# Layer 0 of a four-layer AdaLN/FFN kernel: a copy moved to VectorE, constants computed per group, two stores moved, and unread transposes added on TensorE

## The chip, the cores and the metric

The kernel runs on one core of one Trainium2 chip. A core has five engines that run their own instruction streams and wait for one another only through semaphores: TensorE (PE in the profile, with its weight loads as a row of their own, PEld), VectorE (DVE), ScalarE (ACT), GpSimd (POOL) and SyncE (SP). SP, ACT and POOL also issue DMA transfers. The metric is the device time of one execution in microseconds; lower is better. A difference under about 0.3% (5.7 us here) can't be told from no change.

## The reference

Four layers follow one another, each `x = x + ffn(cond(x))`, with x of 32 sequences x 64 positions x 256 features, so 2048 rows. All data are float32. The change touches layer 0 alone:

```python
def _L0_cond_ref(hidden_states, activation, W_q, b_q, W_kv, b_kv, no_op_k, no_op_v, W_proj, b_proj):
    q = hidden_states @ W_q + b_q                      # heads: 16 of 16 features
    kv = activation @ W_kv + b_kv                      # one key and one value per sequence
    k = concatenate([no_op_k, k1]); v = concatenate([no_op_v, v1])
    w = softmax(einsum('bhsd,bhkd->bhsk', q, k))       # two keys only
    return einsum('bhsk,bhkd->bhsd', w, v) @ W_proj + b_proj

def _L0_ffn_ref(x, router_w, router_b, w1, b1, w2, b2):
    gates = softmax(x @ router_w + router_b)           # 8 experts, the best 2 of each row
    # each expert takes at most capacity = 320 rows, in the order of the rows
    out = gelu(rows @ w1[e] + b1[e]) @ w2[e] + b2[e]
    y = sum over experts of gate * out
```

There are only two keys per head, so the softmax depends on one difference: score = q . (k1 - no_op_k). With W_q folded into that difference, it is x . A plus a constant per sequence and head, where the constant is b_q . (k1 - no_op_k).

## The kernel before

A library schedules the program: it follows the program order and dependencies with its own estimate of the times and writes a fixed order for each engine; within that order every engine waits for what it needs. `tc.issue_after(mark)` adds one rule: what is traced in its block on the engine of `mark` is placed behind `mark` in that engine's order. It is an order of issue, no wait.

Layer 0 runs in these stages. `constants` (L148) makes the identity and turns the condition rows; SiLU of them is the first thing that ACT computes. `fold_loads` (L675) and the loop at L829 issue the first loads: Wq, Wkv and the four pieces of X (512 KB each) from ACT, the small ones from SP. The hardware transfers use eight completion counters in turn, and an issue waits until the last user of its counter has landed.

`fold_scores` (L704) makes `kx`, the key differences spread over heads (L736), turns Wq with four transposes (`transposed`, L119, called at L743), copies the turned leaves out of the PSUM bank (`wqT`), multiplies them with `kx` into A (L752), and computes the constants of all four groups of rows at once with sixteen narrow matmul records (L758) into `z0`. The same loop then makes `vx` for the values. `evacuate` (L106) gives its copies to ACT and to DVE by turns; the count runs through the first three layers.

Then comes a loop over four groups of four tiles of 128 rows (L833): X is turned (`tile_features`, L127, copies on ACT), the scores are made by L841, `z0` is added on DVE (L846, L847), and the weights `at_w` follow by two exponentials on ACT and four DVE instructions. `fold_output` (L780) folds W_proj and the router into `M` (wpT copied by `evacuate`, L791, L796, L801, L809).

The next loop over groups (L858 on) makes the rows of the table: matmuls L866 and L867, a copy to C on ACT (L868), the softmax of the gates on DVE, and a store of 528 KB per group from SP (L872). Behind the loop in program order SP stores X into `acc` (L878, 2048 KB, and L879, 128 KB), and ACT fills `acc_c` with zeros (L884, 2176 KB). Nothing ties these three to the table loop, so the scheduler issued them as soon as X had landed.

`routed` (L451) runs the experts. `slots` (L361) finds which rows each expert takes: `positions` (L307) by two matmuls, then one-hot planes on DVE (L357) and sixteen narrow fp16 matmuls per expert (L397); ACT writes the row numbers (L401). POOL gathers the expert's rows from the table with indirect DMAs (L473, three per expert), which need all four table stores to have landed; PE turns them (L481), and the expert's matmuls run (L438, L447). While this goes on SP loads pieces of the last layer's weights (L1399, 176 KB each over 88 partitions, and L1403) and later experts' weights.

PSUM holds four one-bank buffers (`bank`) and two of two banks (`wide`); a new tile takes the buffer that was released first.

## Time and profile before

| what | value |
|---|---|
| median of three runs | 1898.23 us (1897.44 to 1902.32) |
| the profiled execution | 1896.54 us, of which the span is 1894.8 us |
| PE busy | 1546.4 us, 82% of the span |
| PEld busy | 1191.3 us, 63% |
| DVE, ACT, POOL busy | 712.0, 600.8, 569.4 us |
| mean granted TensorE clock | 0.873 |
| first matmul of the first expert (L438) | at 74.13 us |
| POOL's first gather from the table (L473) | at 65.75 us |

A row of the timeline reads: start in us, length in us, engine, line, operation, output<-input, shapes, number of merged instructions, and in brackets the idle time before it and what ended that. A q behind an engine's name is its sequencer issuing transfers. A row of a stretch's sums reads: bounds, length, then per engine the busy time and the number of instructions, the granted clock, the DMA engines' busy share and GB/s.

### The profile page before, as it was taken

The numbers are of one execution on the slowest core, as the hardware profiler recorded it, in microseconds if no ns is written. First come the engines' busy times: TensorE is split into PE (matmuls) and PEld (weight loads), VectorE is DVE, ScalarE is ACT, GpSimd is POOL, SyncE is SP. The second block draws the span as 40 slices with busy tenths as digits, with TensorE's granted clock in tenths as the row PEclk, the third lists the DMA queues.
The fourth block names the chain that finished last, engine by engine and source line by source line (L and its number), as shares of the span: only waits on it lengthen the run. The fifth ranks groups of instructions, "written<-read, shape, count | busy, mean of one in ns | idle before, by whom it ended". The sixth has DMA issues, their size and how long they took to land.

```text
span 1894.8 us, 26736 instructions
## 1 busy us (share of the span) xinstructions
PE 1546.4 (82%) x9935; PEld 1191.3 (63%) x9935; DVE 712.0 (38%) x2402; ACT 600.8 (32%) x1308; POOL 569.4 (30%) x740
## 2 busy tenths in 40 slices
PE   6799998999987839999675499999665669878767
PEld 5576767888876738888564366667543446546445
DVE  3782043111101161111213601000456668777765
ACT  2222332333331203333211022222134455545443
POOL 0233310233320013332100223331235445455452
PEclk9799998999997959999885599999867778788789
DMA  7455542566632046666511044442310100100000
GB/s 262 139 153 136 137 117 60 171 194 178 179 95 86 6 157 172 179 181 164 152 26 25 24 107 129 105 112 64 115 32 22 46 17 23 32 14 32 14 12 11
DMA packets 158406, 183.81 MB, mean 97 GB/s; under 512 B 37540, under 2 KB 137536, under 8 KB 158272
## 3 DMA queue, kind: packets, MB, share of 16 engines
q1 hardware_dynamic: 123920, 143.34, 23.7%
q0 software_dynamic: 21248, 29.24, 8.9%
q10 hardware_dynamic: 13104, 9.47, 1.6%
q8 instruction: 81, 1.33, 0.3%
q14 instruction: 53, 0.43, 0.1%
HBM read 152.22 MB, written 29.79 MB: 96 GB/s over the span
## 4 chain that ended last, share of the span: by engine, by line
PE 26%; DVE 9%; POOL 6%; issue 5%; ACT 4%; DMA 1%; SPq 0%; POOLq 0%; DVEq 0%
PE bank L438 6%; PE bank L447 6%; PE bank L1133 3%; PE bank L1877 2%; PE bank L1761 2%; PE bank L1684 1%; PE bank L1894 1%; PE bank L1458 1%; PE bank L1795 1%; ACT squares L1603 1%; PE bank L1596 1%; PE wide L1145 1%; DVE mag L1360 1%; POOL mb_root L147 1%; POOL mag L1353 1%
## 5 line engine op out<-in xcount | busy, mean ns | idle before, releaser
L447 PE MATMUL bank<-w,hidden 128*128 128x256 f32 (+1 forms) x2080 | 458.7, 379 | 0.0
L447 PEld LDWEIGHTS bank<-w,hidden 128*128 128x128 f32 (+1 forms) x2080 | 387.8, 187 | 66.2 <-issue 6.5
L438 PE MATMUL bank<-xeT,w 128*128 128x256 f32 (+2 forms) x1440 | 400.1, 437 | 25.2 <-ACT xeT L110 22.2
L438 PEld LDWEIGHTS bank<-xeT,w 128*128 128x128 f32 x1440 | 275.5, 194 | 137.9 <-issue 65.2
L626 DVE TENSOR_TENSOR y<-bank,b 128x256 f32<-128x256 f32 x58 | 24.6, 425 | 361.0 <-PE bank L447 361.0
L440 ACT ACTIVATE hidden<-bank,ge_cols 128x256 f32<-128x256 f32 x232 | 109.8, 473 | 114.7 <-PE bank L438 114.7
L489 DVE TENSOR_TENSOR y<-bank,b 128x256 f32<-128x256 f32 (+1 forms) x56 | 23.6, 422 | 304.5 <-PE bank L447 304.5
L440 ACT ACTIVATE hidden<-bank,bias_cols_b 128x256 f32<-128x256 f32 (+1 forms) x128 | 73.7, 580 | 122.7 <-PE bank L438 118.3
L491 POOL DMA_INDIRECT acc<-y,l2f_add x32 | 50.6, 1582 | 161.9 <-ACT y L490 91.2
L628 POOL DMA_INDIRECT acc_c<-y,pl_add x30 | 47.8, 1594 | 137.0 <-DVE gate L618 90.7
L628 POOL DMA_INDIRECT acc<-y,pl_add x28 | 44.6, 1592 | 131.7 <-DVE gate L618 93.5
L473 POOL DMA_INDIRECT xg<-table,l2f_read x32 | 36.0, 1125 | 158.1 <-ACT l2f_read L401 148.7
L491 POOL DMA_INDIRECT acc<-y,l0f_add x24 | 38.5, 1605 | 111.6 <-ACT y L490 68.6
L1877 PE MATMUL bank<-wg,yT 128*128 128x352 f32 x128 | 58.4, 588 | 16.2 <-ACT h_glu L1879 6.6
L490 ACT ACTIVATE y<-y,xg 128x256 f32<-128x256 f32 (+1 forms) x56 | 28.4, 508 | 131.8 <-DVE y L489 128.9
L1684 PE MATMUL bank<-wqkv,mo_uT 128*128 128x512 f32 (+1 forms) x128 | 55.7, 588 | 15.2 <-ACT ex L1748 11.7
L438 PE MATMUL bank<-XT,w 128*128 128x256 f32 x256 | 65.5, 412 | 2.0 <-DVE C L921 1.4
L1894 PE MATMUL bank<-wd,hT 128*128 128x256 f32 x192 | 59.6, 450 | 5.5 <-ACT h_glu L1879 2.7
L627 ACT ACTIVATE y<-y,gate 128x256 f32<-128x256 f32 x58 | 29.5, 509 | 106.9 <-DVE y L626 106.9
L1877 PE MATMUL bank<-wu,yT 128*128 128x352 f32 x128 | 54.4, 549 | 9.3 <-DVE h_glu L1881 8.5
L110 ACT COPY xeT<-bank 128x256 f32<-128x256 f32 (+1 forms) x57 | 20.6, 362 | 130.1 <-PE bank L124 88.4
L614 POOL DMA_INDIRECT xg<-table_x,pl_read x30 | 31.8, 1062 | 98.6 <-DVE pl_empty L567 56.5
(586 smaller groups left out, 2468.8 us busy)
## 6 DMA issues: line engine op xcount, KB each, us to landing
w<-in_L_ffn_W_dram SPq DMA_DIRECT2D x44, 1024.0 KB
w<-in_L_cond_ew_dram SPq DMA_DIRECT2D x30, 1024.0 KB
w<-in_L_ffn_w_dram SPq DMA_DIRECT2D x16, 1024.0 KB
ad<-ada SPq DMA_DIRECT2D x64, 128.0 KB
X<-acc SPq DMA_DIRECT2D x12, 512.0 KB
w<-in_L_cond_sw_dram SPq DMA_DIRECT2D x4, 1024.0 KB
ad<-ada SPq DMA_DIRECT2D x64, 64.0 KB
b<-in_L_ffn_b_dram SPq DMA_DIRECT2D x30, 128.0 KB
```

Of the source, the lines that this page charges most:

```text
L438: nc.tensor.matmul(ps[:, :cols], w1[:, c, f * P:(f + 1) * P], xT[:, c, :], start=(c == 0), stop=(c == DC - 1))
L440: nc.scalar.activation(h[:, f, :cols], ps[:, :cols], func, bias=bias[:, f:f + 1])
L447: self.nc.tensor.matmul(ps[:rows, :D], h[:, f, at:at + rows], w2[:, f, :], start=(f == 0), stop=(f == FC - 1))
L473: nc.gpsimd.indirect_dma_start(out=xg[:rows], out_offset=None, in_=table, in_offset=bass.IndirectOffsetOnAxis(ap=indices[e * nchunk + c][0 ...
L491: nc.gpsimd.indirect_dma_start(out=acc, out_offset=bass.IndirectOffsetOnAxis(ap=indices[e * nchunk + c][1][:rows], axis=0), in_=y[:rows], ...
L614: nc.gpsimd.indirect_dma_start(out=xg, out_offset=None, in_=table, in_offset=bass.IndirectOffsetOnAxis(ap=read[:, c:c + 1], axis=0), bound ...
L628: nc.gpsimd.indirect_dma_start(out=acc, out_offset=bass.IndirectOffsetOnAxis(ap=add[:, c:c + 1], axis=0), in_=y, in_offset=None, bounds_ch ...
L1133: nc.tensor.matmul(into[s // steps][q * NB:(q + 1) * NB, at:at + width], state(c), w[:, c, q].rearrange("p m f -> p (m f)"), start=False, ...
L1684: nc.tensor.matmul(ps[:, :hi - lo], uT[:, j, c], K["wqkv"][:, c, lo:hi], start=(c == 0), stop=(c == DC - 1))
L1761: nc.tensor.matmul(ps[rows, h * (HD + 1):(h + 1) * (HD + 1)], ex[rows, r, j * DC + c, odd], V[rows, j, h], start=True, stop=True)
L1877: nc.tensor.matmul(ps[:, :half], yT[:, c], w[:, c, cols], start=(c == 0), stop=(c == DC - 1))
L1894: nc.tensor.matmul(ps[:, :D], hT[:rows, k], self.wd[:rows, k], start=(k == 0), stop=(k == KC - 1))
```

## The change

Five edits in layer 0.

1. The turned leaves of Wq are copied by DVE instead of by `evacuate`. The call no longer counts in `evacuate`'s turns, so each later `evacuate` goes to the other engine than before: the first half of A to ACT, the second to DVE, wpT to ACT, and so on.
2. `z0` for all groups is gone; `fold_constant` makes the constant of one group inside the group loop, with two matmuls (four records), a bank and a DVE copy of its own.
3. The store of X into `acc` is issued on SP right behind the first group's table store, so ahead of the other three in SP's order.
4. The zeros of `acc_c` are issued on ACT behind the last copy to C.
5. `repeat` puts transposes of the identity, whose result nobody reads, into PE's order: 12 behind the condition's turns, 4 behind Wq's, 10 behind the positions, 3 behind each of the first four experts' slot passes, 8 more behind the fourth. They write a bank (later one `wide` buffer) kept for them. The later layer that calls `routed` by position gets none.

```diff
+    def repeat(self, mark, n):
+        with self.tc.issue_after(mark):
+            for _ in range(n):
+                self.nc.tensor.transpose(self.unread[:, :P], self.ident, self.ident)
...
-    def transposed(self, out, srcs):
+    def transposed(self, out, srcs, copy=None):
         ps = self.bank()
         for i, s in enumerate(srcs):
-            self.nc.tensor.transpose(ps[:, i * P:(i + 1) * P], s, self.ident)
-        self.evacuate(out, ps[:, :len(srcs) * P].rearrange("p (n q) -> p n q", q=P))
+            self.last_turn = self.nc.tensor.transpose(ps[:, i * P:(i + 1) * P], s, self.ident).ins
+        (copy or self.evacuate)(out, ps[:, :len(srcs) * P].rearrange("p (n q) -> p n q", q=P))
...
+        self.unread = self.bank()
+        self.repeat(last.ins, 12)
...
+        if not by_position:
+            self.repeat(self.last_count, 10)
...
+                if not by_position and e < 4:
+                    self.repeat(self.slot_pass, 3)
...
+                    if not by_position:
+                        self.repeat(half_pass, 8)
...
             self.transposed(wqT.rearrange("p m (c q) -> p (m c) q", q=P),
-                            [wq[:, c, m * P:(m + 1) * P] for m in range(DC) for c in range(DC)])
+                            [wq[:, c, m * P:(m + 1) * P] for m in range(DC) for c in range(DC)],
+                            nc.vector.tensor_copy)
+            self.repeat(self.last_turn, 4)
...
-            ps = self.bank()
-            for g in range(NG):
-                for m in range(DC):
-                    nc.tensor.matmul(ps[:, g:g + 1], self.of_group(x, m, g), bq[:, m:m + 1],
-                                     start=(m == 0), stop=(m == DC - 1))
-            self.z0 = kp.tile([P, NG], F32, name="z0")
-            nc.vector.tensor_copy(self.z0, ps[:, :NG])
+            self.kx = x
...
+    def fold_constant(self, kp, g):
+        nc = self.nc
+        ps = self.bank()
+        for m in range(DC):
+            nc.tensor.matmul(ps[:, :1], self.of_group(self.kx, m, g), self.cols[:, 8 + m:9 + m],
+                             start=(m == 0), stop=(m == DC - 1))
+        z = kp.tile([P, 1], F32, name=f"z{g}")
+        nc.vector.tensor_copy(z, ps[:, :1])
+        return z
...
                     for t in range(g * GT, (g + 1) * GT, 2):
                         self.tile_features(XT, self.X, t, nc.scalar.copy)
+                    z = self.fold_constant(kp, g)
...
-                    nc.sync.dma_start(table_rows[:, rows_of(g)], C[:, rows_of(g)])
+                    stored = nc.sync.dma_start(table_rows[:, rows_of(g)], C[:, rows_of(g)])
+                    if g == 0:
+                        with tc.issue_after(stored.ins):
+                            nc.sync.dma_start(acc_rows[:, :NT], self.X)
+                            nc.sync.dma_start(acc_rows[:, NT], self.X[:, 0])
...
-                nc.sync.dma_start(acc_rows[:, :NT], self.X)
-                nc.sync.dma_start(acc_rows[:, NT], self.X[:, 0])
...
-            nc.scalar.dma_start(self.accc.rearrange("(t p) d -> p t d", p=P),
-                                zero.unsqueeze(1).to_broadcast([P, NT + 1, D]))
+            with tc.issue_after(copied.ins):
+                nc.scalar.dma_start(self.accc.rearrange("(t p) d -> p t d", p=P),
+                                    zero.unsqueeze(1).to_broadcast([P, NT + 1, D]))
...
+                self.unread = self.wide()
```

## The prediction

> **What bounds the kernel now.** I read the page first, then the timeline of the first 85 us, then the transfers by queue, then sums by stretch for the clock.
>
> ```profile
> span 1894.8 us, 26736 instructions
> PE 1546.4 (82%) x9935; PEld 1191.3 (63%) x9935; DVE 712.0 (38%) x2402; ACT 600.8 (32%) x1308; POOL 569.4 (30%) x740
> PEclk9799998999997959999885599999867778788789
> ```
>
> PE is the busy engine, and from the first expert on it runs almost without a break to the end of layer 0. So whatever moves L438's first start moves the end by as much, and the change is worth what it does to that start (74.13).
>
> ```profile
> 1.82 10.64 ACTq L830 DMA_DIRECT2D X<-in_x_dram  x4
> 13.78 0.22 ACT L176 ACTIVATE siluT<-bank 128x64 f32<-128x64 f32 x1
> 13.90 0.58 ACT L110 COPY wqT<-bank 128x512 f32<-128x512 f32 x1
> 14.54 3.78 PE L752 MATMUL bank<-kx,wqT 128*128 128x256 f32 x8 [4.66 <-ACT wqT L110]
> 18.11 3.41 PE L758 MATMUL bank<-cols,kx 128*128 128x1 f32 x16
> 21.39 1.89 PE L730 MATMUL bank<-condT,wkv 128*128 128x32 f32 x8
> 23.09 1.95 PE L132 MATMUL bank<-ident,X 128*128 128x128 f32 x8
> ```
>
> ACT is held by the issues of X until 12.46, then loads a table; the wqT copy stands behind that and PE waits 4.66 us. PE then runs A, the constants and vx without a break.
>
> ```profile
> 38.27 0.68 DVE L112 COPY wpT<-bank 128x512 f32<-128x512 f32 x1
> 39.05 1.03 PE L791 MATMUL bank<-wr,wpT 128*128 128x8 f32 x8 [2.34 <-issue]
> ...
> 51.23 5.31 SPq L872 DMA_DIRECT2D table<-C  x3
> 56.78 1.82 SPq L1399 DMA_DIRECT2D w_q<-in_L_ffn_w_gate_dram  x3
> 58.85 0.39 SPq L872 DMA_DIRECT2D table<-C  x1
> ```
>
> ```profile
> 65.75 2.30 POOL L473 DMA_INDIRECT xg<-table,l0f_read  x1 [61.59 <-DMA w_q<-in_L_ffn_w_up_dram]
> 72.21 1.56 PE L481 MATMUL bank<-ident,xg 128*128 128x128 f32 x6 [2.97 <-DMA xg<-table,l0f_read]
> 74.13 11.01 PE L438 MATMUL bank<-xeT,w 128*128 128x320 f32 x32 [0.35 <-ACT xeT L110]
> ```
>
> The table loop's pace is DVE's (softmax of group 0 at 49.82, flags of group 3 at 59.98). The first gather needs the row numbers (ACT, 65.44) and all four table stores; by the trace's completion counts the last store, issued at 58.85, landed at 64.05. So both paths to the gather are within 1.4 us of each other.
>
> **The change, part by part.** The sum is against the profiled execution, 1896.54 us, of which the span is 1894.8; the median shown is 1.69 above it. I call the first table store's issue T (51.23) and split the sum there.
>
> *The head, up to T.*
> (a) wqT by DVE. DVE ends kx at 10.51 and is then nearly idle, so the copy (0.69, as A's half) would be done at 11.2. But the spare bank is one of the four that PE's early tiles need. Released first are the bias rows' bank (taken by Wq's turns), then the condition's, and that one only when siluT has run, at 14.00. A's first half will take it and start at 14.06 instead of 14.54: -0.5. If it gets another bank: 11.2, -3.3. If Wq's turns themselves take the condition's bank, turns and copy (1.09 + 0.69) follow 14.00: L752 at 15.8, +1.2. I take -0.5, by the order of releases.
> (b) The constants leave the row between A and vx: 21.39 - 18.11 = -3.3.
> (c) Clock. The granted clock's first event in the trace is at 27.27; the page draws full clock before it, but the durations say half: eight transposes took 1.95 us at 23.09, seven took 0.98 at 27.40. With A, vx and X's turns closer together and from 14.06 on, I expect full clock from about 17: vx 1.89 to 0.95, X's turns 1.95 to 1.0, A's tail and group 0's scores another 1.0: -2.9. Bounds 0 and -3.5.
> (d) Per group four records and a DVE copy (0.16). A record of L758 took 0.21 at half clock, so 0.43 to 0.85 a group; PE waits for ACT's XT copies there, which hide most. But a group now takes four banks of four, so its scores wait for the group before to release. Bounds 0 and +3.4 (all records on the path at half clock); I take +1.0.
> (e) wpT goes to ACT, idle from 35.82, instead of behind DVE's queue: the copy could end near 36.8, L791 start 2.2 earlier. L793 behind it is on DVE, and if it stays behind the last reciprocal nothing is won. Bounds 0 and -2.2; I take -1.0.
> (f) After the pause at 36.7 to 39.05 the granted clock is at half from 40.92 to 44.33 (1.7 us lost). With less pause perhaps not: 0 to -1.7, I take -0.85.
> Sum: -0.5 - 3.3 - 2.9 + 1.0 - 1.0 - 0.85 = -7.5, with 4 and 11 as ends that I would still believe. T comes at 43.7.
> Two edits cost nothing here: the 12 turns (12 x 0.213 = 2.6 us at half clock) end by 6.5, before the rows that L717 waits for (6.85); the 4 end long before 14.06.
>
> *From T to L438.* Here SP's queue decides.
>
> ```profile
> DMA packets 2277, 2.32 MB, mean 386 GB/s; under 512 B 15, under 2 KB 2277, under 8 KB 2277
> q1 hardware_dynamic: 1262, 1.29, 60.5%
> q10 hardware_dynamic: 1015, 1.02, 48.1%
> ```
>
> These are the transfers of 22 to 28 us, when the X store (SP, q1) and the zeros (ACT, q10) ran beside each other: together 386 GB/s, in about equal parts. On SP's queue they land in the order of issue: the store of X issued at 16.83 landed at 30.75, and the weights behind it at 34.60, 37.55 and 40.42. Before, both stores ran at 13 to 31 us, while nothing urgent waited; after, they fall between the first table store and the gather. Issued at T: table 528 KB, X 2048 + 128, table 528, table 528, three w_q of 176 (SP issued them ahead of the last table store before, at 56.78), table 528: 4816 KB. The zeros, issued about T + 6.1 (the last copy to C ends at 57.35), share the engines and put all their 2176 KB in between. That is 7.16 MB at 386 GB/s = 18.5 us, + 0.8 because w_q uses 11 engines of 16, + 1.7 for start and landing (T to 54.36 for a first store of 1.4 us). The same count for table, three w_q and table from 56.1 gives a landing at 62.8 where it was 64.05, so + 1.2: T + 22.2. Before, the gather was issued at T + 14.52; now at T + 22.5: +8.0. Behind it the same w_q and wd pieces compete as before. POOL's first two gathers took 2.30 and 2.11, the third 0.97; if DVE's one-hots slow them, they are gone by now, -2.4. A further share of the remaining weights could cost +2. So +5.6 to +10, and I take +8.0. The SP issue of the last table store also waits for the X store's counter, T + 10, which is hidden, since the queue holds it longer.
>
> *The turns from T on.* 10 turns (2.1 us at half clock) end before the first one-hot (63.99 in the time of before); the 3s and the 8 lengthen PE's passes, which end about T + 21 at worst, before the gather lands at T + 28. On the path: 0; without the late gather, up to +0.7. PE then stands still for some 8 us before L481, so L438 starts at half clock as before (4.34 us until 78.47), and the turns save nothing.
>
> ```profile
> 928.40:931.80 3.40, 3.40 (x18) 3.40 (x17) 2.01 (x4) 2.39 (x4) 0.00 (x0) 0.50 1.09 392
> 931.80:935.20 3.40, 3.40 (x68) 2.24 (x70) 2.69 (x5) 2.20 (x4) 0.00 (x0) 1.00 1.04 399
> ```
>
> Can turns hold the clock at all? From 928.40 to 931.80 PE ran nothing but transposes (L1101), at half clock, and from 931.80 the clock is full: they can. The Trainium skill, "TensorE: Matmul & The Clock Gate", section "Part 4: PE-mode transpose", says the opposite, that transposes don't count as busy to the gate. By the page the turns are worth nothing anywhere, by the row up to 2.2 us (half of the 4.34) where they end next to L438 and the gather is not late. Since the gather comes late either way, my sum is the same by both.
>
> *Elsewhere.* `evacuate`'s parity flips through layers 0 to 2; each expert's copies come in both kinds (372 ns on ACT, 424 on DVE) and end together, so 0, bounds -1 and +2. Later scatter-adds need the X store at 89.89 only.
>
> Sum: -7.5 + 8.0 = +0.5; 1897.0 as a profiled execution, 1898.7 as a median. The difference to no change is far under 0.3% (5.7 us).
>
> **Rivals.**
> *Transfers are hidden (faster).* The gather isn't held: the scheduler puts X and zeros elsewhere, or the queues run better than 386 GB/s. Then the head's 7.5 stays, and the turns may bring 2.2: 1898.2 - 9.7, about 1889. Against it: landings in order of issue, and bytes that don't vanish. It decides where the last store lands before T + 16.
> *Slower: the queue outweighs the head.* The place is the last table store behind X, zeros and w_q; the price is +10 when the gather also meets the leftover weights. It decides from a head of 4.3 us or less (10 - 5.7), so if A starts at 15.8 or the groups pay for their fourth bank: about 1905.
> *Nothing earlier in the head at all* is unlikely: (b) alone removes 3.3 us from PE's unbroken row.
>
> **How the numbers follow.** Forecast (the two sides cancel within 5.7): 0.69. Hidden transfers, faster: 0.13. Queue outweighs, slower: 0.18. The forecast's own range goes from a head of 10 with +6 to a head of 5 with +9.5: 1894 to 1903. The range takes in the slower rival and part of the faster: 1891 to 1906.
>
> **What would show it.** Right: L752 at about 14.06 and no L758 row; first table store at 41 to 47; the X store behind it on SP; the last table store landing some 22 us after the first one's issue; POOL's first gather waiting for a DMA and not for ACT; L481 after a PE pause of several us; L438 between 72 and 77, at half clock. Wrong if the gather is issued within 16 us of T, or the head gains under 4 or over 11.

## The result, and the profile after

The changed kernel takes 1915.3 us (median of four, 1912.13 to 1916.14) against 1898.1 us for the kernel before: ratio 1.0083, 95% interval 1.0064 to 1.0101. I had forecast no change, 1898.7 us in a range of 1891 to 1906. The profiled executions are 1916.14 and 1896.54 us; the difference of their spans, 19.6 us, is what the traces have to explain. In the changed kernel all lines stand lower: L752 is L767, L730 is L743, L132 is L138, L796 and L809 are L816 and L829, L872 is L893, L878 and L879 are L897 and L898, L884 is L909, L1399 is L1425, L473 is L487, L438 is L450, L447 is L459, and the new unread turns are L118.

The page of the changed kernel, the same three lines as shown of before:

```profile
span 1914.4 us, 26838 instructions
PE 1563.7 (82%) x9981; PEld 1205.1 (63%) x9981; DVE 707.2 (37%) x2405; ACT 601.0 (31%) x1308; POOL 568.7 (30%) x740
PEclk9699997999996959999885599999876778788788
```

PE is busy for 17.3 us longer. The 46 extra records are the unread turns (12 + 4 + 10 + 4 x 3 + 8), 9.8 us at the 0.213 that one takes at half clock. The other 7.5 us fit a lower clock for the same matmuls: the mean granted clock is 0.865 instead of 0.873, and of the 40 slices of 48 us each, slices 2, 7, 13, 31 and 40 read one tenth lower than before and slice 30 one higher.

I put the start of the same TensorE record side by side in both traces. The offset (after minus before) is -3.1 at the end of the fold of M, +8.1 in the first expert, +8.3 at 269 us, +15.3 at 288 us, +15.4 at 1308 us and +19.0 at 1880 us. So there are four places: the head, the first gather, the start of layer 1, and layer 3.

*The head*, PE's timeline of the changed kernel:

```profile
14.06 1.11 PE L130 MATMUL bank<-ident,wq 128*128 128x128 f32 x4 [5.15 <-ACT siluT L184]
...
15.96 3.29 PE L767 MATMUL bank<-kx,wqT 128*128 128x256 f32 x8
...
19.89 1.07 PE L138 MATMUL bank<-ident,X 128*128 128x128 f32 x8
...
35.83 2.13 PE L816 MATMUL bank<-wpx,cols 128*128 128x264 f32 x4 [1.32 <-DVE wpx L813]
...
38.46 5.80 PE L829 MATMUL bank<-wpx,vx 128*128 128x264 f32 x16
```

Wq's turns themselves now wait for siluT, whose bank they took, and A (L767) starts 1.42 later than before (14.54). X's turns are 3.20 earlier (23.09 before): the constants are out of the row and the clock is full from 18.61 on. At L816 the fold is 4.66 earlier (40.49 before), but its 16 records for M take 5.80 instead of 4.59, mostly at half clock (35.67 to 42.50), so only 3.1 us are left when the table begins.

*The first gather*. SP's issues, in the timeline:

```profile
48.17 0.37 SPq L893 DMA_DIRECT2D table<-C  x1
48.58 0.51 SPq L897 DMA_DIRECT2D acc<-X  x1
49.13 3.06 SPq L898 DMA_DIRECT2D acc<-X  x1
52.30 2.66 SPq L893 DMA_DIRECT2D table<-C  x2
...
60.42 10.05 SPq L1425 DMA_DIRECT2D w_q<-in_L_ffn_w_up_dram  x3
70.58 0.39 SPq L893 DMA_DIRECT2D table<-C  x1
```

X's 2048 KB (L897) go out right behind the first table store. Seven w_q stand ahead of the last table store, and SP needs 15.5 us to issue them (three took 1.82 before). What SP waited for from 50 to 75 us, in the view of waits (us in total, times, longest):

```profile
SPq L1425 <- DMA acc_c<-zero: 6.8, 1, 6.8
```

The seventh of these w_q needs the completion counter that the zeros hold, which ACT had issued at 53.16. By the counter's updates the zeros' last piece landed at 70.16; the w_q was issued at 70.18 and the table store behind it at 70.58. That store landed at 74.5, and then POOL and PE follow:

```profile
75.42 1.35 POOL L487 DMA_INDIRECT xg<-table,l0f_read  x1 [71.25 <-DMA table<-C]
...
79.25 1.43 PE L495 MATMUL bank<-ident,xg 128*128 128x128 f32 x4 [9.89 <-DMA xg<-table,l0f_read]
...
81.89 11.32 PE L450 MATMUL bank<-xeT,w 128*128 128x320 f32 x32 [0.43 <-issue]
```

ACT had the first row numbers at 61.95. The gather comes 27.25 us after the first table store's issue T, where it came 14.52 after it before; the first expert starts 7.76 later than before, at half clock.

*Layer 1*. DVE's timeline before:

```profile
264.87 4.54 DVE L930 TENSOR_REDUCE part<-XT 128x64 f32<-128x1344 f32 x3
276.41 0.29 DVE L1081 CAST b_cut<-b 96x256 bf16<-96x256 f32 x1 [7.00 <-DMA b<-in_L_cond_b_dram]
276.62 0.21 DVE L934 TENSOR_TENSOR agg<-part,part 128x64 f32<-128x64 f32 x1
```

and DVE's and PE's after:

```profile
285.51 0.29 DVE L1107 CAST b_cut<-b 96x256 bf16<-96x256 f32 x1 [12.54 <-DMA b<-in_L_cond_b_dram]
...
286.38 4.52 DVE L956 TENSOR_REDUCE part<-XT 128x64 f32<-128x1344 f32 x3
...
291.03 0.20 DVE L960 TENSOR_TENSOR agg<-part,part 128x64 f32<-128x64 f32 x1
...
292.12 0.80 PE L974 MATMUL bank<-gw,agg 128*32 128x4 f32 x12 [5.79 <-DVE agg L964]
```

The three sums over XT stood ahead of the cast of `b`; now they stand behind it. The cast waits for the loads of `b` (for layer 2), DVE stands still for 12.54 us with the sums ready to run, and PE, which finished L459 at 286.33, waits 5.79 us and goes on at half clock.

### The profile page after: what moved, and what is told of

Its sections match the earlier page's. It is cut to its first block, busy times and chain, and to the rows that moved or that the text cites. A ratio compares the mean times of both kernels' runs of the same rounds, so it can differ in the third digit from the quotient of the medians.

```text
span 1914.4 us, 26838 instructions
## 1 busy us (share of the span) xinstructions
PE 1563.7 (82%) x9981; PEld 1205.1 (63%) x9981; DVE 707.2 (37%) x2405; ACT 601.0 (31%) x1308; POOL 568.7 (30%) x740
## 3 DMA queue, kind: packets, MB, share of 16 engines
q8 instruction: 81, 1.33, 0.3%
## 4 chain that ended last, share of the span: by engine, by line
PE 27%; DVE 8%; POOL 6%; issue 5%; ACT 4%; DMA 1%; SPq 0%; POOLq 0%; DVEq 0%; ACTq 0%
PE bank L450 6%; PE bank L459 6%; PE bank L1159 3%; PE bank L1787 2%; PE bank L1903 2%; PE bank L1710 1%; PE bank L1920 1%; PE bank L1484 1%; ACT squares L1629 1%; PE bank L1845 1%; PE bank L1622 1%; PE wide L1171 1%; POOL mag L1379 1%; PE bank L1821 1%; POOL mb_root L153 1%
## 5 line engine op out<-in xcount | busy, mean ns | idle before, releaser
L459 PE MATMUL bank<-w,hidden 128*128 128x256 f32 (+1 forms) x2080 | 458.7, 379 | 0.0
L459 PEld LDWEIGHTS bank<-w,hidden 128*128 128x128 f32 (+1 forms) x2080 | 387.8, 187 | 66.2 <-issue 6.5
L450 PE MATMUL bank<-xeT,w 128*128 128x256 f32 (+2 forms) x1440 | 401.7, 438 | 23.5 <-ACT xeT L110 22.5
L450 PEld LDWEIGHTS bank<-xeT,w 128*128 128x128 f32 x1440 | 275.8, 194 | 137.4 <-issue 63.6
L487 POOL DMA_INDIRECT xg<-table,l2f_read x32 | 36.1, 1129 | 158.3 <-ACT l2f_read L413 148.8
L1710 PE MATMUL bank<-wqkv,mo_uT 128*128 128x512 f32 (+1 forms) x128 | 57.3, 601 | 16.5 <-ACT ex L1774 13.9
L450 PE MATMUL bank<-XT,w 128*128 128x256 f32 x256 | 67.5, 422 | 0.4 <-DVE C L947 0.4
```

The costliest lines, as they stand in the source:

```text
L450: nc.tensor.matmul(ps[:, :cols], w1[:, c, f * P:(f + 1) * P], xT[:, c, :], start=(c == 0), stop=(c == DC - 1))
L459: self.nc.tensor.matmul(ps[:rows, :D], h[:, f, at:at + rows], w2[:, f, :], start=(f == 0), stop=(f == FC - 1))
L487: nc.gpsimd.indirect_dma_start(out=xg[:rows], out_offset=None, in_=table, in_offset=bass.IndirectOffsetOnAxis(ap=indices[e * nchunk + c][0 ...
L1710: nc.tensor.matmul(ps[:, :hi - lo], uT[:, j, c], K["wqkv"][:, c, lo:hi], start=(c == 0), stop=(c == DC - 1))
```

## The experiments

T is the issue of the first table store, "expert" the first start of L450 (L438). The offsets are the starts of the same record less those of before, at 288, 1308 and 1880 us of before. The ratios are against the kernel before on the same chip. Every other column comes from one profile of each kernel, and one execution differs from the next: five programs that agree on every engine up to T (after, after_again, after_flip, agg_first, agg_wq) have T from 46.97 to 48.23, and best5, best5_again and best5_pad, the same program up to T, from 42.60 to 45.13. A difference in T of a microsecond or two between two kernels is not an effect by itself.

| kernel | T | gather | gather - T | expert | at 288 | at 1308 | at 1880 | ratio (95% interval) |
|---|---|---|---|---|---|---|---|---|
| before | 51.23 | 65.75 | 14.52 | 74.13 | 0 | 0 | 0 | 1 |
| after | 48.17 | 75.42 | 27.25 | 81.89 | 15.35 | 15.37 | 18.98 | 1.0083 (1.0064 to 1.0101) |
| after_again | 48.23 | 75.50 | 27.27 | 81.96 | 15.56 | 16.12 | 19.05 | 1.0086 (1.0069 to 1.0104) |
| agg_first | 47.54 | 74.99 | 27.45 | 81.49 | 7.31 | 6.97 | 10.62 | 1.0039 (1.0026 to 1.0052) |
| after_flip | 47.50 | 74.77 | 27.27 | 81.26 | 7.41 | 6.17 | 6.25 | 1.0034 (1.0023 to 1.0046) |
| wq_evac | 49.53 | 76.61 | 27.08 | 83.06 | 12.64 | 11.87 | 13.48 | 1.0050 (1.0033 to 1.0066) |
| moves_alone | 52.61 | 79.43 | 26.82 | 85.84 | 12.16 | 15.79 | 15.83 | 1.0055 (1.0037 to 1.0074) |
| agg_xback | 48.45 | 74.36 | 25.91 | 80.81 | 6.34 | 7.57 | 8.91 | 1.0036 (1.0023 to 1.0049) |
| agg_wq | 46.97 | 66.18 | 19.21 | 75.02 | 0.70 | 2.46 | 3.40 | 1.0011 (0.9998 to 1.0024) |
| agg_zback | 49.71 | 64.92 | 15.21 | 76.60 | 3.68 | 5.30 | 6.56 | 0.9988 (0.9976 to 1.0000) |
| agg_stores | 46.89 | 61.26 | 14.37 | 69.48 | -6.25 | -4.20 | -3.16 | 0.9968 (0.9953 to 0.9982) |
| z_once | 48.26 | 62.62 | 14.36 | 71.10 | -2.58 | -5.28 | -3.84 | 0.9983 (0.9969 to 0.9998) |
| agg_noturn | 47.69 | 74.80 | 27.11 | 81.31 | 6.48 | 6.85 | 7.69 | 1.0031 (1.0018 to 1.0044) |
| best1 | 47.20 | 61.60 | 14.40 | 70.09 | -2.36 | -3.15 | 3.12 | 0.9994 (0.9977 to 1.0012) |
| best1_noturn | 50.53 | 64.94 | 14.41 | 73.42 | 0.05 | 2.43 | 3.47 | 0.9987 (0.9969 to 1.0004) |
| best3 | 49.20 | 63.56 | 14.36 | 72.97 | -0.68 | -1.39 | 2.04 | 0.9986 (0.9971 to 1.0000) |
| best4 | 43.69 | 58.04 | 14.35 | 66.10 | -9.03 | -9.74 | -3.71 | 0.9960 (0.9945 to 0.9974) |
| best5 | 43.56 | 57.91 | 14.35 | 65.99 | -9.02 | -7.91 | -6.45 | 0.9948 (0.9927 to 0.9969) |
| best5_again | 42.60 | 56.97 | 14.37 | 66.23 | -9.36 | -10.67 | -7.61 | 0.9956 (0.9943 to 0.9970) |
| best5_pad | 45.13 | 59.49 | 14.36 | 68.78 | -6.86 | -8.00 | -4.68 | 0.9957 (0.9942 to 0.9972) |

### Layer 1: an order on DVE

**agg_first** puts one cast behind the aggregate, and nothing else:

```diff
-                nc.vector.tensor_scalar(agg[:, i], agg[:, i], 1.0 / n, None, ALU.mult)
+                self.last_agg = nc.vector.tensor_scalar(agg[:, i], agg[:, i], 1.0 / n, None, ALU.mult).ins
...
-            nc.vector.tensor_copy(cut, b)
+            with self.tc.issue_after(self.last_agg):
+                nc.vector.tensor_copy(cut, b)
```

> The kernel after, with one constraint of order more: the first cast of b (L1107) may be issued only after the last scaling of agg (L964). In the profile of after, DVE stood still for 12.54 us at that cast, for a transfer of b that landed at 285.5, and the three sums over XT that PE's L974 needs stood behind it; PE waited 5.79 us. Theory 'order on DVE': with the cast behind agg, L974 follows the 64 matmuls of L459 with less than 1 us between (they ended at 286.33), and L450 behind it runs at full clock again: layer 1 starts 7 us earlier than in after, 1908 us (1906 to 1911). Rival 'the late start itself': the 7 us come from what follows from the late first gather (weights and b that land later, a cold clock), so that PE pauses about as long whatever DVE's order is: 1915 us (1912 to 1917). Until 260 us both expect the trace of after, with L450's first start at 81.9.

Measured: 1907.77 us, ratio 1.0039. The offset is 7.1 at 83 us and 7.3 at 288 us: the 7 us are gone, and PE's L974 follows L459 without a pause (285.12). The order on DVE is the cause, and the late start is not.

Where did the order come from? **after_flip** keeps the whole change and shifts the alternation of the copies; **wq_evac** takes only the first edit back:

```diff
 # after_flip
     def layer1(self, keep):
+        self.turn += 1
 # wq_evac
-                            [wq[:, c, m * P:(m + 1) * P] for m in range(DC) for c in range(DC)],
-                            nc.vector.tensor_copy)
+                            [wq[:, c, m * P:(m + 1) * P] for m in range(DC) for c in range(DC)])
```

> The changed kernel, with the alternation of evacuate shifted by one copy at the start of layer 1 and nothing else. In the program DVE's sums over XT then stand ahead of the cast of b again, as before the change. Theory 'alternation': the 7.0 us at the start of layer 1 go, the offset to before stays near 8 from 83 to 350 us, ratio 1.003 to 1.005. Rival 'the late start': the 7 us stay, ratio 1.008.

> The changed kernel with its first edit taken back: the copy of Wq's turns goes through the alternation again (to ACT). Theory 'alternation': every copy behind it is on the engine of before, DVE's order at layer 1 is that of before, the 7 us go: ratio 1.003 to 1.005. The edit itself saved nothing in the head by this theory: Wq's turns end at 15.1 and wait for siluT in both, ACT is idle by then, so A starts at 15.8 to 16 (15.96 in after). Rival 'DVE's copy is what the head gained': A starts at 16.5 or later and the head loses 0.5 us or more against after.

Measured: after_flip 1905.75 us, ratio 1.0034, offset 6.7 at 83 us and 7.4 at 288 us. wq_evac 1910.64 us, ratio 1.0050; the wait for agg is 0.53 instead of 5.79, but the next 32 records of L450 behind it ran at half clock (10.17 against 7.17 for the 32 ahead of it), so its offset still rises from 9.3 to 12.6. In both the sums stand ahead of the cast. So the first edit, one copy fewer in the alternation, shifted which engine makes each later copy, and with it the estimates of the library that plans the order (the planner), until instructions of DVE far away changed places. The two runs show that the order hangs on the alternation; the way through the planner's estimates is inferred. A shift alone is not enough: with after_flip's line in the kernel before, the program keeps the sums ahead of the cast (no run of it). In the head the first edit saved nothing: A starts at 15.90 with the copy on ACT and at 15.96 with it on DVE.

### The two moved stores

The next variants all contain agg_first's constraint, so that layer 1 is out of the way. **agg_stores** has both stores back where they were. **moves_alone** is the reverse, the kernel before with the two moves only. **agg_xback** and **agg_zback** put X's store, or the zeros, back alone. **agg_wq** leaves both late and lets the weights go only after the last table store:

```diff
 # agg_stores (agg_xback: the first block; agg_zback: the second)
-                    if g == 0:
-                        with tc.issue_after(stored.ins):
-                            nc.sync.dma_start(acc_rows[:, :NT], self.X)
-                            nc.sync.dma_start(acc_rows[:, NT], self.X[:, 0])
+                nc.sync.dma_start(acc_rows[:, :NT], self.X)
+                nc.sync.dma_start(acc_rows[:, NT], self.X[:, 0])
...
-            with tc.issue_after(copied.ins):
-                nc.scalar.dma_start(self.accc.rearrange("(t p) d -> p t d", p=P),
+            nc.scalar.dma_start(self.accc.rearrange("(t p) d -> p t d", p=P),
...
 # agg_wq, after's moves left in
+                    self.stored = stored.ins
...
-                nc.sync.dma_start(w, I[name].rearrange("(r p) k -> p r k", p=R)[:, r:r + 2])
+                with self.tc.issue_after(self.stored):
+                    nc.sync.dma_start(w, I[name].rearrange("(r p) k -> p r k", p=R)[:, r:r + 2])
 # and the same around the two wd_q loads
...
```

> As agg_first, and X's store and the zeros stand where they stood before the change. SP then issues three table stores, three w_q, the last table store, as before. Theory 'queue': the first table store stays near 48.2, the gather follows at T + 14.5 as before, 62.7, and L450 starts at about 71 instead of 81.9: 11 us less than agg_first, 1897 us (1894 to 1900). Rival 'row numbers and turns': the turns among the counting passes hold PE (the last eleven ended at 69.4) so that L450 can't start before about 75: 1901 us (1899 to 1904). If the two moved stores cost nothing: as agg_first.

> The kernel before, with the two moved transfers alone: X's store behind the first table store, the zeros behind the last copy to C. SP's order from there on is that of after (seven w_q ahead of the last table store), DVE's order at layer 1 that of before. Theory 'queue': from the first table store's issue (51.2) to the gather as in after, 27 us instead of 14.5, so L438 starts at 85 to 87 instead of 74.1: 11 to 13 us slower than before, ratio 1.006 to 1.007. By my prediction's own sum, with three w_q ahead: 8 us, 1.004. If the transfers only hurt because the head is shorter in after: under 6 us.

> As agg_first, with X's store back where it was and the zeros still behind the last copy to C. SP issues all eight w_q and both wd_q ahead of the last table store here. By bytes at the 386 GB/s that the trace of before shows: three table stores 1.58 MB, ten weights 2.16 MB, the zeros 2.18 MB beside them, the last table store 0.53 MB, together 6.45 MB or 16.7 us, and some 2 us to land: the gather at T + 19 to 21 with T at 48.2, so about 68, L450 at 74 to 76: 7 us less than agg_first, 1901 us (1898 to 1906). If X's store alone makes the delay: as agg_stores, 1897. If what counts is the number of weights ahead of the last table store (SP waits for a counter at each issue): not better than agg_first, 1908 or more.

> As agg_first, with the zeros back where they were and X's store still behind the first table store. SP issues all four table stores ahead of any w_q here. By bytes: four table stores and X's, 4.29 MB or 11.1 us, and the last row of table is only ready at about T + 8: the gather at T + 13 to 15, as before the change, L450 near 71: 11 us less than agg_first, 1897 us (1894 to 1901). If X's store alone makes the delay, whatever stands behind it: at T + 20 or later, 1904 or more.

> As agg_first (both moved transfers late), with the w_q and wd_q loads issued only after the last table store. SP's order is then table, X twice, three tables, weights. Theory 'bytes': four table stores, X's and the zeros, 6.47 MB at 386 GB/s are 16.8 us and some 2 to land: the gather at T + 18 to 20, 67 to 69, L450 at 73 to 76, 6 to 9 us less than agg_first (ratio to before 0.9995 to 1.001). Theory 'SP holds the store behind the weights' counters': seven w_q and the counters they wait for made all the delay beyond the first 14.5 us, so the gather goes at T + 15 to 16.5 and L450 at 71 to 73. Rival 'the order of w_q is nothing': as agg_first, gather at T + 27.

agg_stores: 1895.2 us, ratio 0.9968, about 0.3% faster than before, which is the least that can be told. The gather is back at T + 14.37 and the expert starts 12.0 earlier than in agg_first. The rival "row numbers and turns" (no expert before 75) falls. What the gather waits for is now the row numbers: ACT wrote them until 60.95, the gather followed at 61.26, and the last table store had landed at 59.41. moves_alone: ratio 1.0055, T + 26.82; the expert starts 11.7 later than before although the head is 1.4 later at most, so this price belongs to the two moves. (Its ratio is a little under the 1.006 to 1.007 that was expected.)

Which part of it? agg_xback missed my byte count: 6.45 MB should have landed by T + 19 to 21, and the gather came at T + 25.91. Its last table store was issued at 68.36 only, behind ten weights; one of these, a wd_q, waited 3.9 us for the zeros' counter. agg_zback has no zeros in the way and all four table stores ahead of any weight, and T + 15.21. Its profile is of the slowest of its ten executions (1903.73, median 1899.44). There the price turns up later, in gathers that bring their rows slowly beside X's store and the weights (PE waited 1.61 and 1.81 us for them), so that from T to the expert it takes 26.89 where agg_stores takes 22.59. agg_wq is the count by bytes: SP's and POOL's rows of its timeline are

```profile
51.10 4.08 SPq L893 DMA_DIRECT2D table<-C  x3
...
66.18 1.35 POOL L487 DMA_INDIRECT xg<-table,l0f_read  x1 [62.01 <-ACT l0f_read L413]
```

with the gather at T + 19.21, in the range that the bytes gave. The bracket names ACT, but that is its second write of row numbers (65.73 to 66.00), which this gather doesn't need: the first was done at 61.00. The last table store landed at 65.17, and the gather follows 1.01 later; in after and agg_first it follows 0.92 and 0.91 after that landing. So of the 12.7 us by which the gather came later after T, 4.7 remain when the weights stand behind the last table store (19.21 - 14.52): X and the zeros among the table's bytes. The other 8.0 are issue order: seven weights ahead of that store, with their own bytes, and with SP's wait of 6.8 us for the zeros' counter. No run parts these two. The last store on PE's path was held by a transfer on another engine's queue. The rival "SP holds the store behind the weights' counters" had put all of the delay there (T + 15 to 16.5), which is too much.

### The head

**z_once** is agg_stores with the sixteen constant records and one copy between A and vx, as before. **agg_noturn** is agg_first with `range(0)` in `repeat`.

```diff
 # z_once
-            self.kx = x
+            ps = self.bank()
+            for g in range(NG):
+                for m in range(DC):
+                    nc.tensor.matmul(ps[:, g:g + 1], self.of_group(x, m, g), self.cols[:, 8 + m:9 + m],
+                                     start=(m == 0), stop=(m == DC - 1))
...
-                    z = self.fold_constant(kp, g)
+                    z = self.z0[:, g:g + 1]
 # agg_noturn, best1_noturn
-            for _ in range(n):
+            for _ in range(0):
```

> As agg_stores, with the constants computed once between A and vx (16 records and one copy) as before the change. By my prediction's steps the move is worth 3.3 less 1.0 us: X's first turns 3.3 us later than in agg_stores (19.1), T 2.3 us later (49.2), ratio about 0.998. Theory 'same work, other place': at the granted clock of this stretch the 16 records cost 1.7 to 2.4 us wherever they stand (the four per group took 0.50 each in agg_stores), so T moves by less than 1 us: ratio 0.996 to 0.9975.

> As agg_first without any unread turns. By my prediction the turns are worth nothing while the gather is late: L450 at 81 to 82.5 as with them, ratio to before within 0.0008 of agg_first's 1.0039. Theory 'turns hold the clock in the head': as best1_noturn against best1, T is 3.3 us later without them (51.5), and the gather with it: L450 at 84 to 86, ratio 1.0055.

z_once: X's turns start at 22.07 instead of 19.10, 2.97 later (my step said 3.3). The row of the constants itself takes 1.94 of that (19.24 to 21.18); most of the rest is A, which took 3.78 instead of 2.79, since the clock came to full at 19.70 instead of 17.32. T is 1.37 later, between my steps (2.3) and the rival (under 1), which decides nothing: in these two profiles the scores end 5.27 apart and the stretch from L816 to the end of the fold takes 5.16 against 6.85, with the clock. The intervals of the two ratios overlap.

agg_noturn: the expert at 81.31 against 81.49 with the turns, ratio 1.0031 against 1.0039. From T to the expert it takes 33.62 against 33.95, so from T on the turns are worth nothing, as predicted. In the head T is the same too (47.69 against 47.54), but there two effects cancel. PE's timeline of agg_noturn:

```profile
8.67 1.09 PE L130 MATMUL bank<-ident,wq 128*128 128x128 f32 x4
11.68 2.08 PE L767 MATMUL bank<-kx,wqT 128*128 128x256 f32 x4 [1.92 <-DVE kx L749]
```

Without the unread turns, and so without a bank that they hold, Wq's turns don't wait for siluT, and half of A runs at 11.68; the other half waits for siluT until 14.67. X's turns start at 18.11 instead of 20.85. But the clock comes to full at 24.70 instead of 20.48, and the scores end at 33.28 against 33.14. So it was edit 5, by the bank that it keeps, that made Wq's turns wait in the changed kernel.

**best1** to **best5** are agg_stores (with agg_first's constraint) and these edits, on the way to a faster kernel:

```diff
 # best1 (best4 too): the unread turns' tile is a wide one
-        self.unread = self.bank()
+        self.unread = self.wide()
 # best3: best1, and the fold of the output weights ahead of the groups
                 vx = self.fold_scores(kp, loads)
+                self.fold_output(kp, loads, vx)
...
-                self.fold_output(kp, loads, vx)
                 self.more_constants()
 # best4, best5: siluT from SBUF, so that its bank is free at once
-        nc.scalar.activation(self.siluT, view, AF.Silu)
+        nc.scalar.activation(self.siluT, self.condT, AF.Silu)
```

> As agg_stores, and the tile that the first unread turns write is one of the wide ones, so that it takes none of PE's four small banks. In agg_stores Wq's turns waited until 13.76 for siluT, whose bank they took; kx was ready at about 10.4. Theory 'bank': Wq's turns run at about 8.2, A starts at 10.5 to 11.5 instead of 15.66, X's tiles have landed by 16.5, so X's first turns go 3 to 4.5 us earlier and the first table store too: T at 42.5 to 44, L450 at 65 to 67 instead of 69.48, ratio to before 0.9945 to 0.9955. Rival 'Wq's or X's landing': A starts earlier but the turns of X wait, so T moves by less than 1.5 us: ratio 0.996 to 0.997.

> As best1 without any of the unread turns (the loop runs zero times). Theory 'turns hold the clock': in agg_stores L450's 32 matmuls took 8.85 us where they took 11.01 before, with the turns right before them; without the turns L450 starts cold, so 2 us are lost there, and up to 1.5 us more in the head (A at half clock): slower than best1 by 1.5 to 3.5 us. Rival by the rule that turns don't count as busy for the clock: no difference, or faster by the 0.5 to 1 us that the turns hold PE before L495.

> As best1, and the fold of the output weights (wpT, wr's product, M) is issued ahead of the groups' turns instead of behind them. In agg_stores these 10.7 us (32.42 to 43.1) stand between the last scores and the first row of the table, 1.3 us of them waiting for DVE behind the last reciprocal and most of the rest at half clock; put ahead, 5 to 8 us of PE's work moves in front of X's turns, where PE has a pause only until about 11. Theory 'tail': T comes 3 to 6 us earlier than in best1, ratio to best1's 0.997 to 0.9985. Rival 'PE is the bound in the head': the sum of PE's work up to T stays, so T moves by less than 1 us.

> As best1, and siluT is computed from condT in SBUF instead of from the condition's bank. In best1 Wq's turns ran at 8.0, as the theory 'bank' said, but A then waited for the same bank and the same siluT until 14.25. Theory 'bank held by siluT': with the bank free at 4, A starts when kx is ready, at 10.4 to 10.8, and X's first turns go at 14.5 to 15.5 where X's tiles have landed by then (the four loads landed between 12.1 and 16.5 in agg_stores); T at 43 to 45 against 47.2, L450 at 66 to 68, ratio to before 0.9945 to 0.9965. Rival 'X's landing or a cold clock': the 3.6 us are lost again before T, which stays within 1 us of 47: ratio 0.9985 to 1.

> As agg_stores, with siluT computed from condT alone; the unread turns keep their small bank. Theory 'bank held by siluT': the condition's bank is free at 4, so three banks are enough for Wq's turns and A; the trace up to the first table store is as in best4, T at 43 to 45. Rival 'four banks are too few with one kept for the unread turns': some tile still waits for a bank that is released late, and T stays above 46.

best1 fell short: Wq's turns ran at 8.00, but then A's first tile got the condition's bank and waited for siluT until 14.25. That is the start that I had predicted for the change itself (14.06). T did not move (47.20 against 46.89), and the ratio is 0.9994. best1_noturn: T 3.33 and the expert 3.33 later than with the turns. Its A starts earlier (11.64), but its clock comes to full at 30.72 instead of 17.16. So in this pair of profiles the turns are worth 3.3 us, all of it in the head, and in the pair above nothing. The ratio (0.9987) doesn't show it: the two come together again in layer 3, where their offsets are 5.6 us apart at 1308 us and 0.35 at 1880 us. best3 won nothing: PE's 5.94 us for M, now ahead of X's turns at half clock, are not hidden, T is 2.0 later than in best1, and the ratio can't be told from best1's. best4 and best5 remove the cause, siluT's hold on a bank. PE's timeline of best5:

```profile
10.19 3.68 PE L767 MATMUL bank<-kx,wqT 128*128 128x256 f32 x8 [1.27 <-DVE wqT L131]
...
14.52 1.07 PE L138 MATMUL bank<-ident,X 128*128 128x128 f32 x8
...
65.99 8.85 PE L450 MATMUL bank<-xeT,w 128*128 128x320 f32 x32 [0.43 <-ACT xeT L110]
```

A waits only for kx and wqT, T is 43.56, the expert starts 8.1 earlier than before, and at full clock (8.85 for 32 matmuls against 11.01 before). The 2.2 us are the size that my prediction had given the turns by its row, where they end next to the first expert and the gather is not late. agg_stores has them too (8.85), best1 has not, since its clock comes to full at 75.18 only; no pair of runs shows that they come from the turns. One small bank for the unread turns does no harm once siluT holds none. best5 beats both kernels: 0.9948 (0.9927 to 0.9969), and measured again 0.9956 (0.9943 to 0.9970).

### Layer 3: the clock's grid

Between 1308 and 1880 us the changed kernel lost another 3.6 us, though from 1343 us on the order of instructions is the same on every engine in both traces, and between 1300 and 1343 only a few neighbours on ACT and DVE change places. Three kernels speak to this:

```diff
 # best5_pad (after_again and best5_again are the same kernels once more)
-                        self.repeat(half_pass, 8)
+                        self.repeat(half_pass, 16)
```

> The changed kernel itself once more. In its first profile it was 15.37 us behind the kernel before at 1307.9 (time of before), 17.5 at 1409 and 20.3 at 1499, and the granted clock was 0.50 from 1503.5 to 1510.3 where before had 1.00 for the same matmuls. Theory 'execution': how the clock's stretches lie over PE's pauses differs from execution to execution, so the offset at 1307.9 is again 15 (14.5 to 16) and the steps behind it differ by 2 us or more from the first profile's. Rival 'program': +2.2 and +2.8 us again, within 0.5.

> The fastest kernel so far (as agg_stores, siluT from condT), timed in five rounds: ratio to before 0.993 to 0.997. In its profile it was 7.91 us ahead at 1307.9, 5.05 at 1499, 6.45 at 1880. Theory 'execution': other steps between 900 and 1880 this time, by up to 4 us; until 640 the same offsets within 0.5 (-10.3 at 83, -9.0 at 288).

> As best5 with eight more unread turns before the first expert (16 instead of 8), where PE is on the path: L495 followed the turns at once. At half clock they cost 8 x 0.213 = 1.7 us. The order of everything else is that of best5. Theory 'clock stretches': L450 starts 0.9 to 1.7 us later, and the end differs from best5's by anything from -2 to +5 us, since the steps behind 900 fall otherwise. Rival 'a delay stays a delay': the end is 0.9 to 1.7 us later than best5's, ratio to before 0.0005 to 0.0009 higher.

after_again: 1915.94 us, ratio 1.0086. The step from 1470 to 1499 us is +2.7 again (+2.8 in the first profile), and the end is 19.05 again (the step from 1308 to 1409 us is 1.6 instead of 2.2), so my theory of a different step in each execution is not borne out by it; only around 1010 us did the two differ by 2 us. best5_again is 2.8 further ahead than best5 at 1308 us and 1.2 at 1880 us. best5_pad tells little: its T is already 1.6 to 2.5 later than in the two profiles of best5, before the added turns, and its ratio is the same as best5_again's.

What the steps follow was in the traces. All changes of the granted clock in one trace lie on one grid of 3.413 us; the grid's offset against the first instruction differs from execution to execution (1.54 in after, 3.37 in before, 0.25 in agg_stores, 0.02 and 2.61 in the two of best5). I took the position of the same record, the one at 1470 us, within its own trace's grid, for all 20 profiles, beside the step that follows by 1499 us:

| position in the grid (us) | step from 1470 to 1499 us | profiles |
|---|---|---|
| 1.17 to 1.44 | +2.62 to +2.78 | after, after_again, agg_first, wq_evac, agg_xback, z_once, best1, best1_noturn, best3, best4, best5, best5_again, best5_pad |
| 2.07 to 2.35 | -0.01 to +0.06 | before, agg_stores, agg_zback, agg_wq, moves_alone, agg_noturn, after_flip |

What happens there, in the sums by stretch of before (the granted clock is the third number from the end):

```profile
1485.90:1489.30 3.40, 3.40 (x28) 3.03 (x25) 3.23 (x12) 1.89 (x4) 2.80 (x4) 1.00 0.05 17
```

and in the stretch of after with the same work:

```profile
1503.50:1506.90 3.40, 3.40 (x35) 3.00 (x34) 2.35 (x5) 1.98 (x5) 1.62 (x4) 0.50 0.00 0
```

Sixteen matmuls on `ww` (L1819, now L1845) begin in these stretches. They take 3.72 in before and 6.30 in after, because the clock is at half. The step before it goes the same way. From 1340 to 1409 us eight profiles, after among them, lose 1.3 to 1.8 us, and in these the record at 1340 us lies at 2.64 to 3.34 in its grid; in the other twelve it lies at 0.92 to 2.18, and they lose 0.6 at most. So these parts of the loss go with where PE's work lies in the grid, and not with what the change does there. The 1.4 us that after wins back between 1499 and 1880 us were not followed. Why a kernel comes to one position or the other is open: executions with quite different offsets (best5's two) arrive at the same one, and agg_first and after_flip, alike within 1 us up to 1308 us, at different ones.

## Why the prediction was wrong, step by step

**(a) wqT by DVE, -0.5: wrong, +1.42.** The step named the right mechanism (the order in which banks are released) and the other outcome, +1.2, as a bound; I took the wrong one. The bank that tipped it is the one kept for the unread turns, which the step had counted ("the spare bank") and not followed: without it Wq's turns run at 8.67 (agg_noturn), and with the unread turns in a wide buffer at 8.00, with A at 14.25 (best1). The four turns behind Wq's, which were to end long before 14.06, ended at 16.02.

**(b) Constants, -3.3: right.** The row that took 3.28 before is gone from between A and vx. **(c) Clock and (d) records per group: right together.** From L767's start to X's turns it is 3.93 instead of 8.55, that is -4.62, of which 3.28 are (b); from X's turns to the end of the scores 12.29 instead of 13.62.

**(e) wpT on ACT, -1.0: nothing won.** The condition that I had written down, L793's copy behind the last reciprocal, came true: from the end of the scores to L816 it is 3.65 instead of 3.78.

**(f) No clock drop, -0.85: wrong, +1.60.** The drop came earlier and for two stretches of the grid (35.67 to 42.50) instead of one (40.92 to 44.33); from L816 to the end of the fold it is 8.43 instead of 6.83. This is the grid in one execution and not the change: after_flip and agg_first, the same program up to T, have one stretch there and take 6.84 and 6.83, and moves_alone, with the head of before, takes 8.01. The term was worth 0, give or take 1.6 by execution.

Head: 1.42 - 4.62 - 1.33 - 0.13 + 1.60 = -3.06, not -7.5. In the five profiles of the same head it is -3.0 to -4.3. The text called itself wrong under 4.

**From T to the gather, +8.0: wrong, +12.73.** The bytes were about right (agg_wq: T + 19.2, where the same count without the three w_q gives T + 20.3). The failed step is SP's order, carried over from before: three w_q ahead of the last table store. There were seven. And I let the counters be "hidden" by pricing X's store alone, when the zeros' counter was the one that SP waited for, 6.8 us. (The 0.8 in that sum, for three w_q on 11 of 16 engines, comes to 0.6 from their 528 KB at 386 GB/s; nothing hangs on it.)

**From the gather to the expert** I had 0 with a bound of -2.4; it is -1.91 (6.47 instead of 8.38). **Turns from T on, 0: right** (agg_noturn). For the head the text had priced the turns at nothing: there they cost a bank and moved the clock, and that the two cancel in agg_noturn is luck. Sum at the first expert: -3.06 + 12.73 - 1.91 = +7.76.

**Elsewhere, parity 0 (-1 to +2): wrong, +7.0.** I priced the flipped alternation by the copies' durations. What it changed was the planner's order on DVE, at layer 1. No step of mine looked at an order that the planner might write anew behind the first expert. With it fell the sentence that the whole sum rests on, that the end moves by as much as the first expert's start: 7.76 there became 19.0 at 1880 us, and agg_stores' 6.25 at 288 us became 3.16.

The rest, 3.6 us between 1308 and 1880, is in layer 3, and the prediction had no term for it. Its two large steps (+1.8 and +2.8) go with the position in the clock's grid.

Of the rivals, "the queue outweighs the head" had the right place, the last table store, and the right condition, a head of 4.3 or less; its price (+10) was 2.7 too low, and 1905 lacks layer 1 and the grid. It should have had more than 0.18, since three of my six terms for the head had their unfavourable case written beside them.

The weighing of the turns against the clock came out on the trace's side. PE's timeline of agg_stores:

```profile
3.69 2.82 PE L118 MATMUL bank<-ident 128*128 128x128 f32 x12
...
7.06 1.08 PE L743 MATMUL bank<-condT,wkv 128*128 128x32 f32 x8
```

The twelve unread transposes ran from 3.69 to 6.51, inside one stretch of the grid (3.66 to 7.08) in which PE did nothing else but three small transposes, and the granted clock was full from 7.08 on. Of the sixteen profiles with the turns, six have the grid so that one stretch holds all twelve (it begins at 3.37 to 3.66), and in all six the clock is full from its end; in the other ten, where the grid cuts the turns, it is not. Two profiles without the turns have the grid at the same place (before 3.37, best1_noturn 3.41), and their clock stays at half until 27.27 and 30.72. The Trainium skill, "TensorE: Matmul & The Clock Gate", "Part 4: PE-mode transpose", says that transposes do not count as busy in the same way; these runs differ from it.

## What to carry to other kernels

A transfer that nobody waits for still holds a place in its issuing engine's queue and one of the completion counters: before moving it, look at which urgent issue will come to stand behind it, and at the issues that will want its counter, on other queues too. In a kernel whose order is planned, an edit that takes one copy out of an alternation can reorder instructions several layers away; compare the issue order of the whole program, not that of the edited part. When a matmul waits for a PSUM buffer, find the last reader that releases it: here it was an activation behind another engine's long issues, and reading its input from SBUF moved the first table store by about 3 us more (46.89 in agg_stores, 43.56 in best5).

## What the runs showed of the hardware that I hadn't expected

- One issue on SP waited 6.8 us for a transfer that ACT had issued, through a completion counter that both engines' transfers use in turn.
- The clock's grid. Its 3.413 us are the same in all 20 traces, its offset anything from 0.02 to 3.41, and at one place in layer 3 a step of about 2.7 us, 0.14% of the kernel, comes or stays away with the position in the grid, in 20 of 20 profiles. The Trainium skill, "TensorE: Matmul & The Clock Gate", "What's actually happening", says that the window is 3413 ns long and free-running, not started by the kernel; the traces agree.
- The turns' worth depends on that offset too: in after (grid 1.54) the same twelve turns were cut by the grid at 4.95, the clock stayed at half, and L743's eight records took 1.92; in agg_stores they fell into one stretch and L743 took 1.08.
